# Masked attention layers: the output projection a pair of steps later, the divided outputs kept in the tile of the spread reciprocals

## The chip, the core and the metric

The kernel runs on one core of a Trainium2 chip. The time is the device time of one execution in microseconds (us), the median of three runs. Five engines work side by side, each through its own instruction queue in order: TensorE (PE: matrix products; its weight loads are listed apart as PEld), VectorE (DVE), ScalarE (ACT), GpSimd (POOL) and SyncE (SP, which here only starts transfers). Engines wait for each other by semaphores.

## The reference

Four cross-attention layers are applied one after the other to x (2048 queries of 256 channels), all with the same context (1601 keys of 512 channels). Layers 0, 2 and 3 are alike, each with its own weights: 16 heads of 64, a bias on four chosen key columns, softmax over the keys, output projection and residual ("masked" layers below). Layer 1 is a grouped-query layer with an RMS norm. Everything is float32. A masked layer, cut to what matters:

```python
q, k, v = x @ Wq, ctx @ Wk, ctx @ Wv            # 16 heads of 64
logits = einsum('bhqd,bhkd->bhqk', q, k) * 64 ** -0.5 + col_bias
probs = softmax(logits, axis=-1)
x = einsum('bhqk,bhkd->bhqd', probs, v).reshape(B, HW, 1024) @ Wo + bo + x
```

## The kernel before

**Tiles.** A masked layer is worked off in 8 blocks of 2 heads; a block in 4 units of 512 queries. There are 96 masked units. A unit goes over the 1601 keys in 13 chunks: 12 of 128 keys and a tail of 65. One chunk of one unit is a step, and the main loop advances by pairs of steps.

**Software pipeline.** Three units are in work at once. In a pair of steps the kernel computes the scores of two chunks of the newest unit (L715 on PE, copied out of PSUM by ACT at L727 and folded into a running maximum by DVE at L730 and L732), subtracts the maxima and takes exponentials of two chunks of the unit before it (DVE L806, ACT L811; POOL adds the exponentials up at L816), and multiplies two chunks of exponentials, which run two steps behind, with the values (PE L851, into the one PSUM tile `po`). When the last chunk of a unit is through L851, ACT copies `po` to `oT` (L873), and only then may L851 of the next unit begin to write `po`.

**Score tiles.** The scores of a chunk lie in a PSUM tile `s` of two banks. There are two such tiles, used in turn; one is free again when DVE has read it (L732). The projection L928 writes its result into the next tile of the same two, and DVE adds it to the residual (L940), which frees it.

**The end of a unit.** `finish` lists what is left, in steps counted from the unit's last value product: at +2 `add_up` (the sum over partitions, PE L884; ACT L888 copies it to the tile `by`, and SP sends it out at L893), at +4 `denominators` (DVE L901 takes reciprocals; SP spreads them over the partitions of `by`, L678 and L681), at +6 `divide` (POOL L920, `oT` times `by`), at +10 `project` (PE L928, DVE L940). The tiles `oT` and `by` exist once each.

**Fill.** The keys (L461, or L548 and L567 for the grouped layer) and values (L415) of the next block are cut into pieces of about 2 us of PE work. `Pieces.pair` runs what is due and as a rule one such piece, at the end of a pair; after a pair that ran `project` or the maxima, it does this at the front of the next pair. So moving `project` also moves fill and `add_up`.

**Order.** The last lines of the function add dependencies that keep PE, ACT and DVE in the order in which they were written. POOL and SP are ordered by the scheduler of the framework.

**Two kinds of stretch.** From one group of L775 (the maxima of a unit, turned for the reduction) to the next, a stretch holds seven pairs or six, in turn, since 13 is odd. With S for the scores of a pair (L715), V for its value products (L851; V' for half of it, one chunk), F for a piece of fill, P for `project`, A for `add_up`, Q for the queries (L485) and T for L775, PE's order in before.py is

```
seven pairs:  F  S V  S V  P F  S V  S V' F V'  S V A  S V Q  S V F  T
six pairs:    F  S V  S V  P F  S V  S V A  S V F  S V Q  T
```

In the fourth pair of the seven, V' is the last chunk of one unit and the V' behind it the first of the next, with L873 between them.

Of the kernel before, what the change touches and what calls it, by code (L numbers as in the profile page):

```python
# [14 lines left out]
ALU = mybir.AluOpType  # L15
# [11 lines left out]
Piece = namedtuple("Piece", "run cost shared", defaults=(True,))  # L27
# [7 lines left out]
def tile_cross_attention_stack(ctx: ExitStack, tc: tile.TileContext, t: dict, out: bass.AP):  # L35
# [33 lines left out]
    nc = tc.nc  # L69
# [614 lines left out]
    class Unit:  # L684
# [232 lines left out]
                    )  # L917

        def divide(self):
            nc.gpsimd.tensor_tensor(self.oT, self.oT, self.by, ALU.mult)  # L920

        def project(self):

# [58 lines left out]
        def finish(self):  # L982

            if self.very_last:
                return [(0, Piece(lambda: self.quarters(of[len(units) - 2]), 2.0))]
            if self.final:

                at = 4 if self.b == NB - 2 else 2
                found = [
                    (at, Piece(self.add_up, 1.0)), (at + 2, Piece(self.denominators, 0.0)),  # L990
                    (at + 4, Piece(self.divide, 0.0)),
                ]
                if self.b < NB - 2:
                    found.append((10 - 2 * self.b, Piece(self.project_rows, 2.0, False)))
                return found
            if not self.masked:
                return [
                    (1, Piece(self.den_columns, 0.0)), (3, Piece(self.denominators, 0.0)),
                    (6, Piece(self.divide, 0.0)), (8, Piece(self.project, 2.0, False)),
                ]  # L1000
            return [
                (2, Piece(self.add_up, 1.0)), (4, Piece(self.denominators, 0.0)),
                (6, Piece(self.divide, 0.0)), (10, Piece(self.project, 2.0, False)),
            ]


# [386 lines left out]
```

## Time and profile before

| what | value |
|---|---|
| runs | 4673.53, 4681.04, 4683.69 us; median 4681.04 us |
| the profiled execution | 4689.89 us, its span 4688.1 us, mean granted clock 0.985 |
| PE busy | 4523.3 us, 96% of the span |
| DVE, ACT, POOL busy | 77%, 69%, 64% |
| masked layers, 163 to 1224 us and 2333 to 4575 us of the span | PE busy 1032.11 of 1061.00 us and 2177.01 of 2242.00 us |
| the projection L928 | 376 products in `s` tiles, 187.0 us, and 89.5 us of idle PE before them |

A line of the profile gives an engine, a line of the kernel, what it writes and reads, and how often. "Idle before" is time in which the engine stood still just before these instructions; behind the arrow stands what ended it. When an instruction waits for several semaphores, the one that came last by the records is named. Ends of matrix products are modelled, so that short waits inside a group can be hidden in its busy time.

### The profile page before, as it was taken

Reading aid. Unit: us, or ns where it says so; the run is one execution under the profiler, and the core shown is the slowest. Engines: PE = TensorE matmul, PEld = TensorE weight load, DVE = VectorE, ACT = ScalarE, POOL = GpSimd, SP = SyncE. Lnnn points to the kernel's source line nnn. Section 1 sums busy time; section 2 is a strip of 40 time slices with the busy share of each in tenths; the row PEclk is TensorE's granted clock in tenths of the full one; section 3 lists DMA queues with packets and bytes.
Section 4 is the critical chain, followed back from the end, with each engine's and each line's share of the span. In section 5 each row is a group of like instructions: output and inputs, shape, how many; then the busy total and the mean of one; then the engine's idle time right before and its main releaser. Section 6 shows DMA issues by size and latency. Waiting matters only on the chain.

```text
span 4688.1 us, 63813 instructions
## 1 busy us (share of the span) xinstructions
PE 4523.3 (96%) x23563; PEld 1866.2 (40%) x23563; DVE 3614.3 (77%) x3672; ACT 3256.5 (69%) x4108; POOL 2983.9 (64%) x1436
## 2 busy tenths in 40 slices
PE   8999999999999999999999999999999999999998
PEld 5444444443333333343344444444434444444432
DVE  5888888888766666652678888888888888888887
ACT  4777777777645555555667777777777777777776
POOL 3788888888720000000578788888888888888887
PEclk9999999999989999998899999999999999999999
DMA  4333333333211000021233333233232333233311
GB/s 152 87 92 82 84 83 83 82 85 79 66 28 39 26 24 21 21 61 30 74 87 81 87 82 86 78 87 88 74 98 82 84 83 84 81 87 81 84 37 37
DMA packets 377251, 338.00 MB, mean 72 GB/s; under 512 B 143781, under 2 KB 332741, under 8 KB 376940
## 3 DMA queue, kind: packets, MB, share of 16 engines
q1 hardware_dynamic: 373670, 328.54, 26.0%
q8 instruction: 186, 3.05, 0.3%
q0 software_dynamic: 1152, 3.28, 0.2%
q10 hardware_dynamic: 2118, 2.10, 0.1%
q14 instruction: 125, 1.02, 0.1%
HBM read 318.49 MB, written 14.69 MB: 71 GB/s over the span
## 4 chain that ended last, share of the span: by engine, by line
PE 77%; POOL 8%; DVE 6%; ACT 5%; issue 3%; DMA 1%; ACTq 0%; SPq 0%; DVEq 0%; POOLq 0%
PE po L851 21%; PE s L715 19%; PE t L746 9%; POOL sums L816 7%; PE pm L461 6%; PE pm L415 6%; PE s L928 4%; ACT p L727 3%; PE pm L485 3%; DVE top L732 3%; PE pm L884 2%; DVE p L806 2%; PE s L775 2%; ACT p L811 1%; DVE top L730 1%
## 5 line engine op out<-in xcount | busy, mean ns | idle before, releaser
L816 POOL TENSOR_TENSOR sums<-sums,p 128x1024 f32<-128x1024 f32 x1145 | 2713.5, 2370 | 569.4 <-ACT p L811 507.9
L732 DVE TENSOR_TENSOR top<-s,top 128x1024 f32<-128x1024 f32 (+1 forms) x1056 | 1290.2, 1222 | 306.8 <-ACT p L727 250.7
L851 PE MATMUL po<-p,v 128*64 128x512 f32 (+3 forms) x8320 | 1500.4, 526 | 7.8 <-ACT oT L873 4.9
L727 ACT COPY p<-s 128x1024 f32<-128x1024 f32 (+1 forms) x1248 | 1220.6, 1017 | 370.2 <-PE s L715 295.9
L806 DVE TENSOR_TENSOR p<-p,b 128x1024 f32<-128x1024 f32 (+1 forms) x1248 | 1471.0, 1208 | 1.4 <-ACT b L801 1.4
L715 PE MATMUL s<-q,kT 64*128 64x512 f32 (+1 forms) x4992 | 1297.1, 626 | 11.3 <-DVE top L732 6.4
L811 ACT ACTIVATE p<-p 128x1024 f32<-128x1024 f32 (+1 forms) x1248 | 1271.7, 1061 | 44.8 <-DVE p L806 44.4
L851 PEld LDWEIGHTS po<-p,v 128*64 128x64 f32 (+3 forms) x8320 | 367.2, 125 | 1132.1 <-issue 939.0
L715 PEld LDWEIGHTS s<-q,kT 64*128 64x128 f32 (+1 forms) x4992 | 405.9, 182 | 719.1 <-DVE top L732 353.3
L833 ACT ACTIVATE p<-t 128x512 f32<-128x512 f32 (+1 forms) x760 | 413.9, 594 | 296.1 <-PE t L821 255.7
L759 DVE TENSOR_REDUCE row_top<-t 128x1 f32<-128x512 f32 x700 | 450.8, 686 | 198.8 <-PE t L821 166.0
L920 POOL TENSOR_TENSOR oT<-oT,by 128x512 f32<-128x512 f32 x111 | 141.0, 1270 | 707.6 <-DMA by<-cols 503.1
L821 PE MATMUL t<-q,kT 32*128 32x512 f32 (+1 forms) x1520 | 489.0, 643 | 0.0
L746 PE MATMUL t<-kT,q 32*128 32x512 f32 (+1 forms) x1880 | 481.9, 553 | 0.0
L415 PEld LDWEIGHTS pm<-wv,ct 128*128 128x128 f32 (+1 forms) x2600 | 304.1, 188 | 82.4 <-issue 42.5
L415 PE MATMUL pm<-wv,ct 128*128 128x128 f32 (+2 forms) x2600 | 324.8, 277 | 2.6 <-ACT v L419 1.4
L461 PE MATMUL pm<-ct,wk 128*128 128x256 f32 (+1 forms) x1344 | 308.0, 372 | 6.2 <-issue 3.3
L461 PEld LDWEIGHTS pm<-ct,wk 128*128 128x128 f32 x1344 | 235.2, 191 | 115.0 <-issue 68.5
L730 DVE TENSOR_TENSOR top<-s,p 128x1024 f32<-128x1024 f32 x96 | 117.6, 1225 | 207.2 <-ACT p L727 207.2
L928 PE MATMUL s<-oT,wo 128*128 128x512 f32 x376 | 187.0, 620 | 89.5 <-POOL sums L816 62.0
L746 PEld LDWEIGHTS t<-kT,q 32*128 32x128 f32 x1880 | 182.4, 185 | 163.8 <-issue 96.7
L419 ACT COPY v<-pm 128x256 f32<-128x256 f32 (+1 forms) x168 | 60.0, 357 | 243.0 <-PE pm L415 243.0
(173 smaller groups left out, 2158.0 us busy)
## 6 DMA issues: line engine op xcount, KB each, us to landing
ct<-ctxT SPq DMA_DIRECT2D x288, 512.0 KB
xT<-xT SPq DMA_DIRECT2D x100, 512.0 KB
spread<-cols SPq DMA_DIRECT2D x96, 512.0 KB
by<-cols SPq DMA_DIRECT2D x190, 128.0 KB
xT<-xs SPq DMA_DIRECT2D x16, 512.0 KB
ct<-ctxT SPq DMA_DIRECT2D x48, 130.0 KB
wk<-in_L_xattn_Wk_dram SPq DMA_DIRECT2D x24, 256.0 KB
wv<-in_L_xattn_Wv_dram SPq DMA_DIRECT2D x24, 256.0 KB
```

Source lines behind the costliest of these rows:

```text
L415: nc.tensor.matmul(pv[:md, d, :f], ct(k)[:, d * P : d * P + md], wv[:, k, :], start=(k == 0), stop=(k == NCT - 1),)
L461: nc.tensor.matmul(pk, u.wk[:, k, :], ct(k), start=(k == 0), stop=(k == NCT - 1))
L715: nc.tensor.matmul(s[:m, h, :], self.u.kT[r, a : a + m], self.q[r, :], start=True, stop=(a != TAIL),)
L727: nc.scalar.copy(p[:m], s[:m])
L732: nc.vector.tensor_tensor(self.top[:m], s[:m], self.top[:m], ALU.max)
L746: nc.tensor.matmul(s[:, at : at + n], self.q[r, ts(q, P)], self.u.kT[r, a : a + n], start=True, stop=True,)
L759: nc.vector.tensor_reduce(self.top[:, of, q, k : k + 1], s, AX.X, ALU.max)
L806: nc.vector.tensor_tensor(self.p[c][:m], self.p[c][:m], self.less[:m], ALU.add)
L811: nc.scalar.activation(p[:m], p[:m], AF.Exp)
L816: nc.gpsimd.tensor_tensor(self.sums[:m], self.sums[:m], p[:m], ALU.add)
L821: nc.tensor.matmul(s[:m], self.u.kT[r, a : a + m], self.q[r, :], start=True, stop=True)
L851: nc.tensor.matmul(to, v, p, start=(c == 0 and not part), stop=(c == NT - 1 and part != 0))
```

## The change

`divide` writes its result into `by` instead of `oT`, and `oT` of the unit then points to `by`. In the masked layers, except in the last block of a layer, `divide` stands at +8 and `project` at +12, one pair of steps later; that is 84 of the 96 masked units. In the last block they stay at +6 and +10 (the last block of layer 3 has a list of its own, which isn't touched, but uses the new `divide`).

```diff
         def divide(self):
-            nc.gpsimd.tensor_tensor(self.oT, self.oT, self.by, ALU.mult)
+            nc.gpsimd.tensor_tensor(self.by, self.oT, self.by, ALU.mult)
+
+            self.oT = self.by
...
+
+            at = 10 if self.u.n == self.layer.BLOCKS - 1 else 12
             return [
                 (2, Piece(self.add_up, 1.0)), (4, Piece(self.denominators, 0.0)),
-                (6, Piece(self.divide, 0.0)), (10, Piece(self.project, 2.0, False)),
+                (at - 4, Piece(self.divide, 0.0)), (at, Piece(self.project, 2.0, False)),
             ]
```

PE's order in the changed program, with the letters from above:

```
seven pairs:  F  S V  S V  F  S V  P F  S V' V'  S V A  S V Q  S V F  T
six pairs:    F  S V  S V  F  S V  P A  S V  S V F  S V Q  T
```

In 40 of the stretches of seven pairs and 41 of those of six the order changes in this way. In three further stretches at the end of layer 3, where there is no fill, only P and A move, or nothing. On POOL the place of L920 among the additions L816 is the same in both programs (behind 7 or 8 of the 12 in nearly all units); on SP one weight load (L450) stands one context load later, and nothing else moves in the regular stretches.

## The prediction

> **What bounds the kernel now.** First the page: PE is busy for 4523.3 us of a span of 4688.1, so at most 165 us can be won by anything that only removes waits.
>
> ```profile
> PE 4523.3 (96%) x23563; PEld 1866.2 (40%) x23563; DVE 3614.3 (77%) x3672; ACT 3256.5 (69%) x4108; POOL 2983.9 (64%) x1436
> L928 PE MATMUL s<-oT,wo 128*128 128x512 f32 x376 | 187.0, 620 | 89.5 <-POOL sums L816 62.0
> ```
>
> More than half of that idle time, 89.5 us, stands before the one line that the change moves. The list of waits of PE splits it into two kinds and shows the next candidate.
>
> ```profile
> PE s L928 <- POOL sums L816: 62.0, 43, 1.4
> PE s L928 <- DVE top L732: 21.6, 45, 0.5
> PE po L851 <- ACT oT L873: 4.9, 5, 1.6
> ```
>
> So 43 waits of 1.44 us (stretches of seven pairs) and 45 of 0.48 us (six pairs). The first kind is put down to POOL, but the timeline of DVE and of PE around one of them says otherwise:
>
> ```profile
> 650.73 3.47 DVE L806 TENSOR_TENSOR p<-p,b 128x1024 f32<-128x1024 f32 x3
> 654.12 2.54 DVE L732 TENSOR_TENSOR top<-s,top 128x1024 f32<-128x1024 f32 x2
> ...
> 652.09 1.94 PE L851 MATMUL po<-p,v 128*64 128x512 f32 x8
> 655.48 1.95 PE L928 MATMUL s<-oT,wo 128*128 128x512 f32 x4 [1.45 <-POOL sums L816]
> ```
>
> POOL's division for this projection ended at 649.84. The first of the two L732 ends at 655.4, and PE starts at 655.48: L928 waits for a score tile, which DVE frees late because three subtractions stand ahead of the maxima. In the six-pair case two stand ahead and the wait is 0.48. What stands behind L928 in both is fill, which needs no score tile.
>
> The last of the views is the end of layer 3, where no fill is left. There the order that the change makes in the seven-pair stretches (last chunk of a unit and first of the next with nothing between) already exists, twice. Timeline of PE and ACT, then a cut into slices of 3.41 us (columns: stretch, its length, busy time and count of PE, PEld, DVE, ACT, POOL, granted clock, DMA share, GB/s); every time at half clock in this trace is one such length or a multiple.
>
> ```profile
> 4511.32 1.08 PE L851 MATMUL po<-p,v 65*64 65x512 f32 x4
> 4514.05 1.08 PE L851 MATMUL po<-p,v 128*64 128x512 f32 x4 [1.65 <-ACT oT L873]
> 4515.06 3.59 PE L715 MATMUL s<-q,kT 64*128 64x512 f32 x8
> 4513.41 0.59 ACT L873 COPY oT<-po 128x512 f32<-128x512 f32 x1
> ```
>
> ```profile
> 576.27:579.69 3.42, 1.98 (x9) 0.56 (x10) 3.32 (x4) 3.42 (x5) 3.26 (x3) 1.00 0.12 47
> 4511.89:4515.30 3.41, 1.76 (x10) 0.44 (x8) 3.31 (x4) 3.06 (x4) 2.91 (x3) 1.00 0.00 0
> 4515.30:4518.71 3.41, 3.41 (x10) 0.89 (x10) 2.32 (x3) 1.01 (x1) 3.09 (x2) 0.50 0.00 0
> ```
>
> PE stood 1.65 us, and in the next slice its clock was halved: eight score products took 3.59 us, not 1.99. The second case (4583.57) is the same. A slice that held a whole wait of 1.44 at L928 was never followed by half clock.
>
> **The change part by part.**
>
> *Six pairs, 41 times.* Before, from the value products at 618.15 to the sixth pair's scores at 637.79: 19.64. After, with spacings from the same stretch: V 1.87, F 1.88, S 1.92, V 1.87, P 1.80, A 0.96, S 1.92, V 1.87, S 1.92, V 1.87, the small F 1.02, together 18.90. Do score tiles come in time? Behind the moved F they do. P needs the first maximum of the third pair: its scores start at 621.9, ACT's copy ends 2.2 later, the maximum takes 1.22, so 625.4, and PE is there at 625.7: no wait, by 0.3. A needs POOL's last addition, which ended at 626.16 in this stretch (four additions, 9.70 from 616.46); A moves from 631.95 to 627.5: no wait, by 1.3. Without fill between the fourth and fifth pair, the second chunk of the fifth waits about 0.15 for its tile. Gain 19.64 - 19.05 = 0.59; 0.55 where the fill is keys, 0.1 slower behind V, and DVE's chain to the end of the stretch moves forward by as much. I take 0.6: 41 x 0.6 = **-24.6 us**. Bounds: the wait alone, 0.48 (-20), and 0.74, all waits in it (-30).
>
> *Seven pairs, 40 times.* Removed: the wait of 1.44 (1.52 counted from where PE is free) and the 0.24 that the fourth pair's scores lose to a late tile (2.23 against 1.99). Added: L851 of the next unit meets L873 with nothing between. From the start of a pair's scores ACT needs 1.23 to begin its copies, 1.81 for them, 0.96 for an exponential, 0.6 for L873: PE goes on at +4.64, and was done at +2.99. That is the row of 1.65. Summed from 652.09 to 668.98: before 16.89; after V 1.87, F 1.92, S 2.02 (0.1 for a late tile), V 1.87, P 1.79, F 1.82, S and V' up to the wait's end 4.64, V' 1.01, together 16.94. So **+2 us** over 40, and the gain of 62 is given straight back. Bounds: 0 (the copy hidden) and 2.0 for the wait, -64 and +16.
>
> *Half clock.* Each slice lost costs 3.59 - 1.99 = 1.60. Two of two stops that lay whole in a slice led to it, so it takes a stop of 1.65 that doesn't straddle a border. If stops fall anywhere, (3.41 - 1.65) / 3.41 = 0.52 of 40, 21 times, +34. But they don't: seven-pair stretches follow each other at 75.84 on average (620.57 to 772.2 is two), and 75.84 - 0.55 is 22.06 slices. The stop then creeps by some 0.2 us each time through the 1.65 in which it straddles (about 8 stretches), is caught once, and the 1.6 lost puts it back near the start of the creep. I take one in 6, between one in 15 and one in 2: 7 x 1.6 = **+11 us**, bounds +4 and +34. The Trainium skill (TensorE: Matmul & The Clock Gate, Part 1: The HAM clock gate) has the same slices of about 3.4 us, but says that the clock falls after at least one idle window of that length. By that rule no stop here would cost clock and this term would be 0; the slice above, 52% busy and followed by 0.50, decides against it.
>
> *Waits of the moved instruction.* L928 waits on DVE and POOL; as it now reads `by`, it also waits for the two transfers that filled it, landed long before (the division waited for them). Each may cost PE's queue one semaphore instruction, 51 ns in the group of L928: 84 x 2 x 0.051 = 8.6 at most, 0 if PE's queue runs ahead of PE. I take **+2**, nearer to 0, since the projection now comes without a wait behind eight products in the queue.
>
> *At no cost.* L920 is the same instruction with another target (1.27 us), at the same place of POOL's order; it ended 5 us or more before the projection, and that now comes later. L873 no longer waits for the projection but for L920, done 17 us before it. L888 of the next unit overwrites `by`, which L928 has read ahead of L884 on PE, so nothing waits anew. On SP, L893 goes out 4.4 us earlier every second unit and L450 one load later; the next transfer that anyone waits for on SP, L893 at 598.75, follows L450 (581.56) by 17 us.
>
> Sum: -24.6 + 2 + 11 + 2 = -9.6 on the profiled execution (4689.9 to 4680.3). That one lies 8.9 above the median of the runs; the work is the same, so I carry the difference to the median: 4681.0 - 9.6 = **4671 us**.
>
> **The rivals.**
>
> *Half clock eats it (slower).* The stop falls anywhere, is caught 21 times: -24.6 + 2 + 34 + 2 = +13, 4694. Place: the V' V' of seven pairs. The balance turns at 13 catches, and 19 make it slower by 0.2%. For: two of two. Against: the creep.
>
> *Both waits simply go.* The copy of `po` would have to be ready in time: 43 x 1.44 + 41 x 0.6 = -86, 4595. Against: twice 1.65 in the same order.
>
> *The wait only moves.* The scores that take the projection's place need the same tile; where no fill is left (three stretches) this is so. If P in six pairs then waits as well and A's earlier place meets POOL late, gains cancel: 4681. A turns into a loss from 1.3 us of lateness on.
>
> **How the numbers follow.** 0.2%, 9.4 us, is about what a measurement of this kernel can tell from no change. The forecast (few catches, 4657 to 4681 by the bounds of its terms) has 0.60; half clock 0.20; both waits gone 0.07; the wait moved or a wait not seen 0.13. The forecast lies at the border of faster and same: of its 0.60, 0.40 faster, 0.19 same, 0.01 slower. Of half clock's 0.20, 0.14 slower, 0.06 same. The third is faster; the last splits into 0.06 same and 0.07 slower. Faster 0.47, same 0.31, slower 0.22. For 8 in 10 the range takes the forecast and half clock's up to its sum and a little noise: 4652 to 4696.
>
> **What would show it.** Idle time before the projection (L930 in the changed kernel) under 5 us. PE's wait for L873 at some 66 us, 40 of 1.6. Seven or so slices at half clock in the masked stretches where there were two. Six pairs at 33.7 us, seven at 41.5. L884's idle time still about 1 us. The prediction is wrong if L873's waits are short, if the slices at half clock number 15 or more, or if the projection still waits.

## The result, and the profile after

The change made the kernel slower by 0.2%: 4686.96 us against 4677.62 us (medians of 20 runs of each kernel), ratio 1.0021 with a 95% interval of 1.0014 to 1.0028. Predicted were 4671 us against 4681, a ratio of 0.998. The profiled execution of the changed kernel took 4684.07 us, its span 4682.2.

First the page and the waits of PE in the changed kernel (columns of the second fence: us in total, times, longest).

```profile
PE 4533.9 (97%) x23563; PEld 1865.7 (40%) x23563; DVE 3615.7 (77%) x3672; ACT 3259.7 (70%) x4108; POOL 2982.4 (64%) x1436
L851 PE MATMUL po<-p,v 128*64 128x512 f32 (+3 forms) x8320 | 1503.7, 526 | 73.7 <-ACT oT L873 70.8
L930 PE MATMUL s<-by,wo 128*128 128x512 f32 x376 | 187.8, 622 | 11.7 <-issue 8.1
```

```profile
PE po L851 <- ACT oT L873: 70.8, 44, 1.7
PE s L930 <- issue: 8.1, 14, 1.4
PE pm L884 <- POOL sums L816: 1.5, 1, 1.5
```

(Lines behind the change are numbered two higher: L930 and L942 are L928 and L940 of the kernel before.) The idle time before the projection went from 89.5 us to 11.7, and most of what is left lies outside the moved stretches. In its place the value products wait 70.8 us for the copy of `po`, 44 times, where it was 4.9 and 5 times. PE's idle time (span less busy time) fell from 164.8 us to 148.3, and yet PE is busy for 10.6 us more than before with the same 23563 products. The timeline of PE around one of the waits shows where that comes from:

```profile
658.79 1.08 PE L851 MATMUL po<-p,v 65*64 65x512 f32 x4
661.52 1.08 PE L851 MATMUL po<-p,v 128*64 128x512 f32 x4 [1.65 <-ACT oT L873]
662.53 3.33 PE L715 MATMUL s<-q,kT 64*128 64x512 f32 x8
```

Eight score products take 3.33 us where 1.99 is usual. All slices at half clock of this trace lie on one grid of 3.413 us. Slices of that length around this stop, and around an equal stop some 455 us earlier (columns as in the prediction: stretch, its length, busy time and count of PE, PEld, DVE, ACT, POOL, granted clock, DMA share, GB/s):

```profile
659.74:663.15 3.41, 1.76 (x10) 0.57 (x10) 3.31 (x4) 2.68 (x4) 2.02 (x1) 0.98 0.17 57
663.15:666.57 3.42, 3.42 (x10) 0.92 (x8) 2.04 (x2) 1.63 (x2) 2.70 (x2) 0.52 0.00 0
202.40:205.81 3.41, 2.62 (x12) 0.58 (x8) 1.82 (x3) 2.66 (x4) 0.11 (x1) 1.00 0.55 154
205.81:209.22 3.41, 2.55 (x12) 0.88 (x12) 3.30 (x3) 2.07 (x4) 2.86 (x2) 1.00 0.00 0
209.22:212.64 3.42, 3.42 (x18) 1.07 (x16) 2.58 (x3) 3.42 (x5) 2.59 (x2) 1.00 0.00 0
```

The stop from 659.9 to 661.5 lies in one slice, which is busy for 1.76 us, and the next slice runs at half clock. The other stop, from 205.0 to 206.7, straddles a border; the two slices are busy for 2.62 and 2.55 us, and nothing follows. (The slices are drawn 0.13 us late: by the clock's own records the slice at half clock is 663.02 to 666.43, which is why the rows show 0.98 and 0.52 and not 1.00 and 0.50.)

The spans of the two profiled executions can't be subtracted as they are: the start and layer 1, which the change doesn't touch, differ by 15 us between them. By stage, in us (cut at the first product of L775 of a unit; sums over the traces):

| part of the program | before | after | slices at half clock |
|---|---|---|---|
| layer 0, 28 stretches | 1059.94 | 1063.37 | 0, then 4 |
| layer 2, 28 stretches | 1073.75 | 1078.28 | 1, then 5 |
| layer 3, 28 stretches | 1061.36 | 1064.80 | 0, then 4 |
| start and layer 1 | 1261.79 | 1246.38 | 35, then 29 |
| between, and end | 231.22 | 229.41 | about 6 in both |

In all, six or seven slices more are at half clock, which at some 1.6 us each is the 10.6 us of busy time. The regular stretches of the masked layers became 11.4 us longer. Kind by kind: a stretch of six pairs went from 34.25 or 34.14 us to 33.99 or 33.89, 0.25 less; one of seven pairs stayed at 41.5 or 41.7, but eleven of them became 43.1 to 43.6, each with one slice at half clock, some 1.65 more. A twelfth such slice lies in the last stretch of layer 0 (38.0, then 39.9). Five more were 0.17 to 0.39 longer, 1.4 us together. 41 x -0.25 + 12 x 1.65 + 1.4 = +11.0 us, which is near the 11.4 by stage and the difference of the medians (+9.3).

Four of these five, and two of the eleven, hold a wait of 0.14 to 0.44 before the moved projection, 1.8 us in all. One of them, on ACT and on PE:

```profile
726.20 1.02 ACT L801 COPY b<-spread 128x1024 f32<-128x1024 f32 x1 [1.28 <-DMA spread<-cols]
730.73 1.95 PE L930 MATMUL s<-by,wo 128*128 128x512 f32 x4 [0.30 <-issue]
```

ACT waited 1.28 us for the transfer that spreads a unit's maxima (a wait of 1.1 to 1.4 stands there in all six, in five of them put down to this transfer; it is 0.15 in the stretch of the timeline above). Its next copies of scores were late, and so was the maximum on DVE that frees the projection's tile: it ended 0.11 us before the projection began. In the stretch of the timeline above it ended 0.29 before, when PE was still busy. So the moved projection gets its score tile only just in time. Why the fifth of the longer stretches took 0.22 more stays open.

### The profile page after: what moved, and what is told of

It reads as the page before. It is cut to its first block, busy times and chain, and to the rows that moved or that the text cites. A ratio compares the mean times of both kernels' runs of the same rounds, so it can differ in the third digit from the quotient of the medians.

```text
span 4682.2 us, 64013 instructions
## 1 busy us (share of the span) xinstructions
PE 4533.9 (97%) x23563; PEld 1865.7 (40%) x23563; DVE 3615.7 (77%) x3672; ACT 3259.7 (70%) x4108; POOL 2982.4 (64%) x1436
## 4 chain that ended last, share of the span: by engine, by line
PE 92%; ACT 4%; DVE 2%; issue 1%; DMA 0%; POOL 0%; ACTq 0%; SPq 0%; DVEq 0%; POOLq 0%
PE po L851 28%; PE s L715 25%; PE t L746 9%; PE pm L415 6%; PE pm L461 6%; PE pm L485 4%; PE s L930 4%; ACT p L727 2%; PE s L775 2%; PE pm L884 2%; ACT p L811 1%; PE t L821 1%; DVE top L732 1%; PE s L821 1%; PE s L746 1%
## 5 line engine op out<-in xcount | busy, mean ns | idle before, releaser
L816 POOL TENSOR_TENSOR sums<-sums,p 128x1024 f32<-128x1024 f32 x1145 | 2713.9, 2370 | 678.0 <-ACT p L811 613.7
L851 PE MATMUL po<-p,v 128*64 128x512 f32 (+3 forms) x8320 | 1503.7, 526 | 73.7 <-ACT oT L873 70.8
L811 ACT ACTIVATE p<-p 128x1024 f32<-128x1024 f32 (+1 forms) x1248 | 1271.6, 1060 | 42.4 <-DVE p L806 42.0
L715 PEld LDWEIGHTS s<-q,kT 64*128 64x128 f32 (+1 forms) x4992 | 415.8, 184 | 687.1 <-DVE top L732 255.6
L920 POOL TENSOR_TENSOR by<-oT,by 128x512 f32<-128x512 f32 x111 | 141.3, 1273 | 702.2 <-DMA by<-cols 416.7
L776 DVE TENSOR_REDUCE ntop<-s 128x8 f32<-128x1024 f32 x96 | 117.5, 1224 | 123.8 <-PE s L775 123.8
L930 PE MATMUL s<-by,wo 128*128 128x512 f32 x376 | 187.8, 622 | 11.7 <-issue 8.1
```

Source lines behind the costliest of these rows:

```text
L715: nc.tensor.matmul(s[:m, h, :], self.u.kT[r, a : a + m], self.q[r, :], start=True, stop=(a != TAIL),)
L811: nc.scalar.activation(p[:m], p[:m], AF.Exp)
L816: nc.gpsimd.tensor_tensor(self.sums[:m], self.sums[:m], p[:m], ALU.add)
L851: nc.tensor.matmul(to, v, p, start=(c == 0 and not part), stop=(c == NT - 1 and part != 0))
```

## The experiments

All ratios are to the kernel before, by runs of it that belong to the kernel in question, with 95% intervals. The medians of these runs were 4682.31 us for the first three kernels below (each kind of stretch alone, the earlier copy) and the division alone, 4674.33 for the later copy, the kept fill, the values first and the move alone, 4678.11 for the control and the fill ahead, and 4676.69 for the last kernel, so that a time below divided by 4677.62 doesn't give its ratio. "Six pairs" and "seven pairs" are the lengths of the two kinds of regular stretches, which were 34.14/34.25 and 41.48/41.70 us before.

**The two kinds of stretch, each alone.** Units end alternately in one kind and the other, so the parity of the unit's index `b` selects it.

```diff
-            at = 10 if self.u.n == self.layer.BLOCKS - 1 else 12
+            at = 10 if self.u.n == self.layer.BLOCKS - 1 or self.b % 2 else 12
```

> The projection is a pair later only where it falls in a stretch of six pairs. Theory: a six-pair stretch wins 0.25 us (as the changed kernel's trace has it: 33.99 and 33.89 us against 34.25 and 34.14), nothing is lost elsewhere, no new slice at half clock: 41 x 0.25 = 10 us faster, ratio 0.998. The prediction's 0.6 would give 25 us, 0.995. If the six-pair part costs something that the lengths of stretches don't show, the ratio is 1.000 or more.

```diff
-            at = 10 if self.u.n == self.layer.BLOCKS - 1 else 12
+            at = 10 if self.u.n == self.layer.BLOCKS - 1 or self.b % 2 == 0 else 12
```

> The projection is a pair later only where it falls in a stretch of seven pairs. Theory: the removed wait of 1.44 comes back as the stop of 1.65 before the next unit's first value product, stretches of seven stay at 41.5 and 41.7 us, and those whose stop lies whole in a 3.41 us slice become 1.65 longer. The stretches now follow each other at 75.84 us, 22.22 slices, so the stop moves 0.75 us each time through a zone of 1.65: about one in three is caught, 11 to 15 of 40, 18 to 25 us slower, ratio 1.004 to 1.005. Rival (the loss lies outside the masked layers, or is noise between runs): 1.000.

Six pairs alone: 4670.99 us, ratio 0.9971 (0.9960 to 0.9983), six pairs 33.9 and 34.0, seven pairs 41.43 and 41.66 (0.045 less than before), no slice at half clock in the regular stretches. Seven pairs alone: 4708.33 us, ratio 1.0041 (1.0027 to 1.0054; the medians alone give 1.0056), six pairs 34.1 and 34.2, seven pairs 41.5 and 41.7, and 17 slices at half clock added in the three layers, some more than expected. They were counted in the profiled execution, which at 4715.27 us was the slowest of the five. So one part of the change wins about 0.25 us per stretch, the other only trades waits and then pays for clock.

**Is the new wait the copy's place on ACT?** In the pair where a unit ends, ACT's order is two copies of scores, an exponential, L873, an exponential. Two kernels move L873 in that order, one exponential earlier and one later, with the rest of the changed kernel as it is.

```diff
+        ends = all(masked(x.valuing) for x in pair) and pair[0].cv == NT - 1
+        if ends:
+            pair[0].valuing.values(NT - 1)
         if masked(pair[0].exping):
             pair[0].exping.masked_exp(pair[0].cb)
         for unit in new:
             unit.maxima_spread()
-
-        ends = all(masked(x.valuing) for x in pair) and pair[0].cv == NT - 1
-        if ends:
-            pair[0].valuing.values(NT - 1)
```

> The changed kernel, but ACT copies po to oT (L873) ahead of the first exponential of that pair, not behind it; PE's order is as in the changed kernel. Theory: the stop shrinks by one exponential, 0.96 us, from 1.65 to 0.7, too short to be followed by half clock. Against the changed kernel 40 x 0.95 + 12 slices x 1.65 = 58 us less, so about 48 us faster than the kernel before, ratio 0.990. Rival (half clock isn't tied to this stop, but to PE's load as a whole): the 12 slices remain, ratio 0.994. Rival (the exponential that now waits makes something else late): no gain, 1.000 or more.

```diff
-        if ends:
-            pair[0].valuing.values(NT - 1)
         if masked(pair[1].exping):
             pair[1].exping.masked_exp(pair[1].cb)
+        if ends:
+            pair[0].valuing.values(NT - 1)
```

> The changed kernel, with L873 on ACT behind both exponentials of that pair, not between them; PE's order as in the changed kernel. Theory: the stop grows by one exponential, from 1.65 to 2.6 us, and a stop needs 1.65 within one slice, so it is caught over a width of 3.41 + 2.6 - 3.3 = 2.7 of 3.41 us: 25 to 35 of 40 slices at half clock where there were 12. Against the changed kernel 40 x 0.95 + 13 to 23 x 1.65 = 60 to 76 us more; against the kernel before 70 to 86 us, ratio 1.015 to 1.018. Rival (half clock isn't tied to the stop's length): 12 slices remain, 48 us slower, 1.010.

The wait for L873, first with the copy earlier, then with the copy later:

```profile
PE po L851 <- ACT oT L873: 31.2, 44, 0.9
```

```profile
PE po L851 <- ACT oT L873: 113.9, 48, 2.6
```

Earlier: 4630.47 us, ratio 0.9885 (0.9870 to 0.9900), seven pairs 40.53 and 40.76, nothing at half clock. Later: 4759.74 us, ratio 1.0177 (1.0156 to 1.0198), seven pairs 42.4 and 42.6, and most of them 1.65 longer still: 35 slices at half clock were added. The stop is set by where ACT's copy stands; a stop of 0.7 to 0.9 us costs no clock, one of 2.6 costs it three times in four. As a control the earlier copy was also put into the kernel before, by the first of these two edits:

> Control: in the kernel before, the copy L873 stands one exponential earlier on ACT, as in the run with that edit on the changed kernel; nothing else moves. My theory: in the kernel before, a piece of fill hides L873, so nothing is won: stretches 34.2 and 41.5 to 41.7 as in before, ratio 0.999 to 1.001. Rival: the earlier copy is a gain of its own (it frees something that both kernels wait for), then the ratio falls to 0.995 or less and the gain of that other run isn't all due to the stop.

4671.74 us, ratio 0.9989 (0.9980 to 0.9998); 81 of the 84 stretches of the table have their length of before to 0.01 us, and the other three, next to layer 1, lost 0.9 us together. The copy's place is worth something only where nothing hides it. The ratio is 0.1% under 1 although the stretches hardly moved, which also tells how far the start and layer 1 can carry a ratio beyond its interval.

**Is it the missing fill between the two value products?** The changed kernel, with the fill kept between V' and V' instead of moved to the front of that pair:

```diff
+        ends = all(masked(x.valuing) for x in pair) and pair[0].cv == NT - 1
-        front = pieces.scored
+        front = pieces.scored and not ends
         pieces.scored = False
```

> The changed kernel, but the pair in which a unit's last chunk meets the next unit's first never takes its fill at its front: the piece of fill stays between the two value products, under L873, and the scores follow the projection directly. Theory: the stop of 1.65 and the slices at half clock go; the second chunk of scores behind the projection waits 0.4 to 0.6 us for its tile, which L942 frees. Seven pairs take 40.2 to 40.5 us: 40 x 1.1 + 12 x 1.65 = 64 us less than the changed kernel, 54 less than the kernel before, ratio 0.988. Rival (a wait only moves: the tile wait comes back whole, 1.4 us): ratio 0.995.

4626.73 us, ratio 0.9894 (0.9875 to 0.9912), seven pairs 40.54 and 40.77, no slice at half clock. The stop is gone; 13.8 us of short waits for the score tile that the projection used take a part of the gain.

```profile
PE s L715 <- DVE xs L942: 13.8, 41, 0.5
```

**The last chunk's products ahead of the scores.** This also gives ACT time, by starting V' one group earlier:

```diff
+        ends = all(masked(x.valuing) for x in pair) and pair[0].cv == NT - 1
+        if ends:
+            pair[0].valuing.values(NT - 1)
         for x in pair:
             if masked(x.scoring):
                 x.scoring.masked_scores(x.ca)
...
-        ends = all(masked(x.valuing) for x in pair) and pair[0].cv == NT - 1
-        if ends:
-            pair[0].valuing.values(NT - 1)
```

> The changed kernel, but in the pair in which a unit ends, the value product of its last chunk stands ahead of the scores of that pair on PE, and L873 ahead of ACT's copies of them. Theory: the scores (1.92 us) now lie between the two value products and cover L873; no stop, no slice at half clock. Seven pairs take 39.8 to 40.0 us: against the changed kernel 40 x 1.6 + 12 x 1.65 = 84 us less, against the kernel before about 74 less, ratio 0.984. Rival (the scores come 0.94 us later, so DVE and ACT are late for the next pair and PE waits there): 0.990 or more.

4637.65 us, ratio 0.9926 (0.9907 to 0.9944). The stop and the half clock are gone, but seven pairs came out at 40.93 and 41.16, not below 40. The waits of PE in this kernel and its timeline behind the second V':

```profile
PE s L715 <- DVE top L732: 40.6, 105, 2.2
```

```profile
655.96 1.08 PE L851 MATMUL po<-p,v 128*64 128x512 f32 x4
657.60 1.13 PE L715 MATMUL s<-q,kT 64*128 64x512 f32 x4 [0.56 <-DVE top L732]
```

In the changed kernel the first of these rows was 8.0 us, 19 times. Scores that start later make the maxima on DVE late, and the next scores wait for their tiles: the rival named there, and the missed half of the forecast.

**The division's target and the place, apart.** First only the division into `by`, with all pieces at their old places; then only the move, with the division into `oT`.

```diff
-            at = 10 if self.u.n == self.layer.BLOCKS - 1 else 12
+            at = 10
```

> Only the division's target is changed: it writes into the tile of the spread reciprocals, the projection stays at +10. Theory: same instruction, same place, the two additional semaphore waits of the projection are hidden: ratio 1.000 (0.999 to 1.001). If each of these waits costs PE 0.1 us as the prediction's upper end had it: 8.6 us slower, 1.002.

```diff
-            nc.gpsimd.tensor_tensor(self.by, self.oT, self.by, ALU.mult)
-
-            self.oT = self.by
+            nc.gpsimd.tensor_tensor(self.oT, self.oT, self.by, ALU.mult)
```

> Only the projection and the division are moved; the division writes into oT as before. Theory: in six pairs L873 now waits for the projection to have read oT, about 0.6 us, but ACT's next work there waits for PE anyway, so nothing is lost: the same stops, 10 to 15 slices at half clock, ratio 1.002 to 1.004. Rival (the tile of the spread reciprocals is what makes the move possible, without it ACT falls behind in every six-pair stretch): 41 x 0.6 = 25 us more than the changed kernel, 1.007.

The division alone: 4675.95 us, ratio 0.9981 (0.9972 to 0.9990), a little faster where no change was expected. All but one of the 84 stretches are 0.045 us shorter, 83 x 0.045 = 3.7 us of some 9, for a reason that stays open (one at the start of layer 2 is 2.1 longer, with a second slice at half clock); the rest lies in parts that vary as in the control above and stays open too. The move alone: 4683.56 us, ratio 1.0017 (1.0008 to 1.0027), the lengths of stretches of the whole change and eleven added slices at half clock where that had twelve. So the result comes from the move, not from the tile that is written.

**The wait before the projection taken away in place.** The kernel before, with the piece of fill that stood behind the projection put ahead of it; this leaves the fill between V' and V':

```diff
-            self.scored = False
+            self.scored = self.swapped = False
...
         def pair(self, steps, pairs):
 
+            if self.swapped:
+                self.swapped = False
+                return self.own(steps)[0] + 1.0
+            due = [p for step in self.due if step <= max(steps) for p in self.due[step]]
+            self.swapped = bool(self.fill) and any(p.cost == 2.0 and not p.shared for p in due)
+            if self.swapped:
+                self.fill.popleft().run()
+                return self.own(steps)[0]
             cost, taken = self.own(steps)
```

> The kernel before, with the projection left a pair of steps where it was, but the piece of fill that stands behind it put ahead of it; divide as before. The fill takes 1.9 us and so covers the waits of 1.44 and 0.48, the fill between V' and V' stays, so there is no stop and no slice at half clock in the regular masked stretches. My theory: PE's waits before L928 fall from 89 us to under 10; the scores right behind the projection now need the tile that it wrote, and wait some 0.4 us (2.4 instead of 1.99) for L940. Seven pairs 41.7 - 1.5 + 0.4 = 40.6, six pairs 34.2 - 0.5 + 0.2 = 33.9, together 40 x 1.1 + 41 x 0.3 = 56 us, ratio 0.988. If a switch between half-array and whole-array groups costs about 0.1 us, the groups show it here: fill behind V 1.98, the projection behind fill 1.8, scores behind the projection late by no more than their tile, and the six pairs gain at least as much as in the kernel with only the six-pair part of the change (0.25). Rival: the late tile takes everything back (the scores wait for L940 by 1.2 us or more, and DVE falls behind): seven pairs at 41.4 or above, ratio 0.998 or more.

4655.87 us, ratio 0.9958 (0.9944 to 0.9971), between the two theories, since the two kinds of stretch went different ways: seven pairs 40.28 and 40.51 as expected (1.2 less), six pairs 34.84 and 34.95 (0.7 more, where 0.3 less was expected). 40 x -1.2 + 41 x 0.7 = -19 us. Timeline of PE in a stretch of six pairs:

```profile
612.18 2.05 PE L415 MATMUL pm<-wv,ct 128*128 128x128 f32 x16
614.07 1.88 PE L928 MATMUL s<-oT,wo 128*128 128x512 f32 x4
615.88 1.13 PE L715 MATMUL s<-q,kT 64*128 64x512 f32 x4
617.27 1.13 PE L715 MATMUL s<-q,kT 64*128 64x512 f32 x4 [0.26 <-DVE xs L940]
618.33 1.94 PE L851 MATMUL po<-p,v 128*64 128x512 f32 x8
620.66 1.13 PE L715 MATMUL s<-q,kT 64*128 64x512 f32 x4 [0.39 <-DVE top L732]
621.99 1.13 PE L715 MATMUL s<-q,kT 64*128 64x512 f32 x4 [0.20 <-DVE top L732]
```

Behind the projection the second half of the scores waits for its tile in both kinds; only in six pairs do two pairs without fill follow each other, and the lateness goes on into the second.

**Each kind of stretch with its better order.** The previous edit for the projections in stretches of seven pairs, the move with the division into `by` for those in stretches of six.

```diff
-            at = 10 if self.u.n == self.layer.BLOCKS - 1 else 12
+            at = 10 if self.u.n == self.layer.BLOCKS - 1 or self.b % 2 else 12
...
-                (at - 4, Piece(self.divide, 0.0)), (at, Piece(self.project, 2.0, False)),
+                (at - 4, Piece(self.divide, 0.0)),
+                (at, Piece(self.project, 2.0 if self.b % 2 else 1.9, False)),
```

> Each kind of stretch gets the order that was better for it: seven pairs the fill ahead of the projection at its old place, six pairs the projection a pair of steps later with the division into by. My theory: the two parts add, since each kind of stretch keeps its own length: seven pairs 40.3 to 40.5 (1.2 less than before), six pairs 33.9 to 34.0 (0.25 less), no slice at half clock in the regular masked stretches: 40 x 1.2 + 41 x 0.25 = 58 us, ratio 0.986 to 0.989. Rival: the state of DVE and of the score tiles at the end of one stretch carries over into the next, as the 0.7 that the six pairs lost in the run with the fill ahead in both could be the tail of a seven: then the six pairs come out at 34.5 or above and the ratio at 0.993 or above.

4609.82 us, ratio 0.9856 (0.9840 to 0.9872), the fastest of all: seven pairs 40.28 and 40.51, six pairs 33.89 and 34.00, no slice at half clock in the regular stretches. The parts add, and nothing carries over from one kind of stretch into the other. The waits that are left at the score tile:

```profile
PE s L715 <- DVE xs L942: 10.8, 42, 0.3
```

## Why the prediction was wrong

The prediction said 10 us faster; the kernel is 9 us slower. What happens was foreseen nearly step by step; two terms of the sum had the wrong size, and the second mostly because of the first.

**Six pairs: -24.6 predicted, -10 measured. This is the first step that failed.** The wait of 0.48 went, and neither the projection nor `add_up` met a late tile or a late POOL, as foreseen. But the sum of spacings, 19.05 us from the value products to the sixth pair's scores, is 19.39 in the changed kernel (611.97 to 631.36); the spacings that I had taken from the old neighbours don't hold beside the new ones. Timeline of PE before and after:

```profile
620.57 1.96 PE L928 MATMUL s<-oT,wo 128*128 128x512 f32 x4 [0.48 <-DVE top L732]
622.37 1.95 PE L415 MATMUL pm<-wv,ct 128*128 128x128 f32 x16
624.24 1.99 PE L715 MATMUL s<-q,kT 64*128 64x512 f32 x8
```

```profile
613.84 2.05 PE L415 MATMUL pm<-wv,ct 128*128 128x128 f32 x16
615.82 1.99 PE L715 MATMUL s<-q,kT 64*128 64x512 f32 x8
617.74 1.94 PE L851 MATMUL po<-p,v 128*64 128x512 f32 x8
619.60 1.98 PE L930 MATMUL s<-by,wo 128*128 128x512 f32 x4
621.52 1.08 PE L884 MATMUL pm<-sums,ones 128*64 128x512 f32 x4
622.53 1.99 PE L715 MATMUL s<-q,kT 64*128 64x512 f32 x8
```

From start to start the projection takes 1.80 ahead of fill and 1.92 ahead of `add_up`, the fill 1.87 behind the projection and 1.98 behind value products, `add_up` 0.96 and now 1.01. The remaining 0.09 is the fifth pair's scores, whose second chunk comes 0.24 late for its tile where I had put 0.15 (2.16 from start to start, not 2.07). The weight loads of PE at the same places, before and after, show what the extra tenth is:

```profile
621.94 0.19 PEld L415 LDWEIGHTS pm<-wv,ct 128*128 128x128 f32 x1 [0.24 <-issue]
622.37 1.75 PEld L415 LDWEIGHTS pm<-wv,ct 128*128 128x128 f32 x15 [0.24 <-issue]
```

```profile
613.83 1.86 PEld L415 LDWEIGHTS pm<-wv,ct 128*128 128x128 f32 x16 [0.81 <-issue]
619.60 0.30 PEld L930 LDWEIGHTS s<-by,wo 128*128 128x128 f32 x2 [0.81 <-issue]
```

Behind the projection, which like the fill uses the whole array (128*128), the fill's first weights are loaded at 621.94, 0.43 ahead of its first product. Behind the value products (128*64) the load begins only with the group itself, at 613.83 and 619.60, after 0.81 in which no weights were loaded. The kernel before had the two whole-array groups side by side and paid for one change into that form and one out of it; the change sets them apart, and each pays its own. In the run with the fill ahead of the projection they are side by side the other way round, and take 1.89 + 1.81 = 3.70 together, against 1.80 + 1.87 = 3.67 before and 1.98 + 1.92 = 3.90 apart. That run had been expected to show 1.98 for the fill behind the value products; it showed 1.89, so the tenth is seen only where a group has another form on both sides, and the sum of the two groups is a better witness than either. That the load can't run ahead across a change of form fits what the Trainium skill says (TensorEngine Tiling (Array Packing), Tiling Modes, Key Properties): a change of tiling mode drains TensorE. The rows agree, at about 0.1 us for a change (3.90 less 3.67 or 3.70 is 0.2 for two changes more). I had seen this tenth for the keys behind V and charged it there alone. That the change of form is the cause was read from the rows; no run measured it by itself.

**Half clock: +11 predicted for seven catches, +20 measured for twelve.** The mechanism was right: every added slice at half clock stands behind a stop at L873, and each costs about 1.65 (1.60 predicted). The count failed: the creep of 0.2 us was worked out with a gain of 0.55 in the six pairs. (The prediction's 75.84 for two stretches was off too: its own rows, 620.57 and 772.15, give 75.79.) With the measured gain the same argument comes near the count: two stretches now take 75.46 or 75.59 in turn, 75.53 on average, which is 22.13 slices of 3.413, so that the stop creeps by 0.44 us each time, not 0.2. The 1.65 lost by a catch leaves 3.41 - 1.65 = 1.76 us of creep until the next one, 1.76 / 0.44 = 4 stretches: 10 in 40, where eleven were counted in the seven pairs. With seven pairs alone two stretches take 75.74, 22.19 slices, the creep is 0.64 us and a catch is due every 2.7 stretches, 15 in 40; 17 were counted. By this argument the less the six pairs win, the more the seven lose.

**Seven pairs: right.** Predicted was no change but for the clock, the wait of 62 us before the projection against stops of 1.65 at L873: 41.47 and 41.70 after, 41.48 and 41.70 before, and 42 of the 44 waits at L873 are of 1.6. (The four parts given there for ACT add up to 4.60 and not 4.64; the other 0.04 lies between the end of the copy and the start of PE.) That the stop is the copy's place on ACT, and not the missing fill as such, was shown from both sides.

**The moved instruction's waits: +2 predicted for semaphores, nothing or a slight gain measured** (0.045 us less per stretch in the run with the division alone). `add_up` met no late POOL: one wait of 1.5 in all, as before. The idle time before the projection was to be under 5 us and is 11.7; within the moved stretches it is the 1.8 us of late tiles shown above, which the sum did not have.

**From the profiled execution to the median.** The prediction carried its 8.9 us above the median over unchanged. Where they lay isn't shown, since one execution of that kernel was traced; start and layer 1 alone differ by 15 us between the two traces. The change is about as large in the medians (9.3) as in the regular stretches (11.4).

**The rivals.** "Half clock eats it" held: its turning point of 13 catches was worked out with a gain of 24.6; with a gain of 10 it is 6. "Both waits simply go" needs the copy to be ready; the run with the earlier copy, where a stop of 0.7 is left, goes that way (0.9885). "The wait only moves" is true of the seven pairs alone.

**The rule weighed in the prediction.** The Trainium skill's rule (TensorE: Matmul & The Clock Gate, Part 1: The HAM clock gate), that the clock falls after at least one idle window of about 3.4 us, would have made this term 0. The runs decide against it: slices that were busy for about half (1.76 of 3.41 us) were followed by half clock.

## What to carry to other kernels

Before work is moved, ask what it was hiding at its old place: here the fill between two products hid a copy. A stop of 1.65 us that lay whole in a clock slice cost its own length and as much again in clock, one of 1.44 only itself, so shortening a wait below that border wins more than the time cut from it. Take the length of a group of products from a row with the same neighbours on both sides, and where a loop has two kinds of passes, cost and change each by itself: the best kernel here used a different order for each.

## What the hardware showed that was not expected

**The border of half clock is sharp.** In the changed kernel and the one with seven pairs alone, 84 stops of 1.6 us were sorted by how far behind a line of the 3.413 us grid of the clock's records they began. Of the 34 at 0.25 to 1.86 us all but one (at 0.25) were followed by one slice at half clock; none of the 50 others was. In the kernel with the move alone the twelve that were followed began at 0.33 to 1.81, and no other stop of 1.6 began there. The 44 stops of 1.4 us in the kernel before, anywhere in the slice, never were, not even where one slice was busy for only 1.97 us; nor were the stops of 0.7. Of 43 stops of 2.6 us, 32 were; the other eleven began at 2.28 to 2.59, where neither of the two slices holds more than about 1.6 of them. All of this fits one rule, read from these counts: a slice in which PE stands for about 1.6 us (between 1.44 and 1.64) is followed by one at half clock, if the lines between slices are taken some 0.3 us later than those of the clock's records.

**A change of the products' form goes with about 0.1 us more of TensorE** at each border between groups that use half the columns of the array (128\*64) or half its rows (64\*128) and groups that use all of it, by the rows above (3.67 and 3.70 us against 3.90). No run here measured it by itself.

**About one more semaphore instruction for each projection cost nothing that could be measured.** With the division alone PE has 232 of them at the projection's line instead of 108, of 51 ns in the median, and the stretches became 0.045 us shorter.
